# Quantizing the last two weight strips half by half, and another order of ScalarE's and GpSimd's work per strip

## The chip, the cores and the metric

The kernel runs on one core of one Trainium2 chip. The metric is device time in microseconds (us) of one execution, the median of three runs. Engines are called TensorE (PE in the profile, with PEld for its weight loads), VectorE (DVE), ScalarE (ACT), GpSimd (POOL) and SyncE (SP, which issues most DMAs). Each engine works through its own instructions strictly in the order in which they were emitted: an instruction that waits holds up everything behind it on its engine.

## The reference, cut to what matters

```python
delta = lora_B @ lora_A * 0.5                        # rank 64
scale = exp(scale_log)
normalized = ((weight + delta).reshape(O, 16, 128)) / scale
cb = codebook / max(abs(codebook), 1e-8)             # 32 entries
idx = searchsorted((cb[:-1] + cb[1:]) * 0.5, normalized, side="left")
quantized = cb[idx]
w_q = ((quantized - normalized) + normalized) * scale
w_eff = w_q + delta
h = x @ w_eff.T                                      # x: 4096 x 2048
out = x + h @ W_base.T + b_base + mixture_of_low_rank_experts(h)
```

All is float32. The kernel never forms `h`. It multiplies the quantized weight with `W_base` (and with the small router and low-rank matrices) first, and then applies the combined 2048 x 2048 matrix to `x`.

## The kernel before, in words

**Stage A** (lines 390 to 870) makes the combined matrix. The quantized weight is worked in 16 strips of 128 input columns; a strip is a tile `w` of 128 x 2048 numbers, two halves `f` of 1024. For one strip `i`:

- `delta(i, f)` (line 405): TensorE makes the low-rank half into PSUM tile `d`. There is one such tile, so the second half waits until ScalarE has read the first.
- `scaled(i, f)` (line 502, ScalarE) copies `d` into `a`, scaled. `normalize(i, f)` (lines 506 and 429, GpSimd) adds it to `w` and divides by the scale. So `w` is normalized in place, and must have been loaded first (`load_w`, line 395).
- The 31 thresholds are climbed one by one; at each, `a` is raised where `w` is above the threshold. The lowest four levels are prepared one strip ahead: `scalar_level` (lines 516, 519, 521 or 524, three ScalarE steps called parts 0, 1, 2) does level 0 of both halves and level 3 of half 0; `pool_levels` (lines 534, 535, GpSimd) does levels 1 and 2 (and level 3 of half 1 for strips 1 to 5); `last_level` (line 539) adds ScalarE's level 3.
- From strip 6 on a first half-size mask (level 3 of half 1) is left to the strip itself. Then come 27 full masks, r = 4 to 30. `raise_to` (lines 549, 550): ScalarE writes a mask `above`, VectorE copies the next level into `a` where the mask is set (COPY_PREDICATED). There are four mask tiles, so ScalarE can be at most four masks ahead.
- `straight_through` (lines 572 to 574): three element-wise passes over each half on GpSimd; for the last strip on VectorE, in quarters.
- `products(i, bs, c)` (line 621) multiplies the strip with a quarter `c` of two column blocks of `W_base` on TensorE; `multiply_router`, `router_sum`, `route` are small matmuls; `keep(i, b)` (lines 654, 655) lets ScalarE empty a PSUM bank and SP store it. Three PSUM banks (tag `m`) serve these products. One strip's products run while the next strip is quantized.

The order of all this is written by hand: in iteration `i` of the strip loop, `behind(k, f, ...)` puts a step into the program right after full mask number `k` (0 to 26) of strip `i`. That fixes its place in the order of each engine that it uses. In iteration `i` the steps for strip `i+1` (scaled, normalize, levels), the products of strip `i-1` and the last quarter of strip `i-2` are placed in this way. For strips 5 to 15 GpSimd also makes sums of finished blocks (`outer_w`, `inner_pair`) that SP stores (`put`).

After the loop the last strip's products, the last stores, and sums of the last group (`late_columns` and then `last_outer`, `last_inner` on VectorE, with GpSimd issuing their DMAs) follow.

**Stage B** (from line 873) is 196 product steps on TensorE of some 7 us each, and takes the rest of the time. It begins with VectorE still working on the last group's sums.

In the profile lines are those of the helper, not of the place in the order. The places are these, for a normal strip:

```python
behind(4, scaled, i + 1, 0)
behind(4, normalize, i + 1, 0)
behind(10, scaled, i + 1, 1)
behind(10, normalize, i + 1, 1)
for r, f, parts in ((0, 0, (11, 12, 13)), (NL - 1, 0, (14, 15, 18)), (0, 1, (19, 20, 21))):
    for n, p in enumerate(parts):
        behind(p, scalar_level, i + 1, f, r, n)
behind(14, pool_levels, i + 1, 0)
behind(19, last_level, i + 1, 0)
behind(21, pool_levels, i + 1, 1)
```

Of the kernel before, what the change touches and what calls it, by code (L numbers as in the profile page):

```python
# [13 lines left out]
U8 = mybir.dt.uint8  # L14
I32 = mybir.dt.int32
AF = mybir.ActivationFunctionType
# [5 lines left out]
P = 128  # L22
BIG = 3.0e38

GAIN = 2.0**126
# [158 lines left out]
def adaln_ffn_kernel(  # L184
# [181 lines left out]
    with ExitStack() as sa:  # L366
# [145 lines left out]
        def scalar_level(i, f, r, part):  # L512
# [9 lines left out]
            elif part == 2:  # L522
                strips[i]["lx"] = mpool0.tile([P, NM // 2, P], F32, tag="lx", name=f"lx_{i}_{f}")
                nc.scalar.activation(strips[i]["lx"], sg, AF.Copy, scale=rise[:, r : r + 1])

        def half_step(i):
            return i - 1 in made

# [12 lines left out]
        def new_mask(i, r):  # L541
            return mpool.tile([P, F], F8, tag="above", name=f"above_{i}_{r}")

        def raise_to(i, r, above, f, n):

            c = ts(f, F // n)
            q = strips[i]["w"].rearrange("p m i -> p (m i)")[:, c]
            a = strips[i]["a"].rearrange("p m i -> p (m i)")[:, c]
            nc.scalar.activation(above[:, c], q, AF.Relu, bias=neg_t[:, r : r + 1], scale=GAIN, saturate=False)  # L549
            nc.vector.copy_predicated(  # L550
                a, above[:, c].bitcast(U8), step[:, r : r + 1].to_broadcast([P, F // n])
            )

        def quantize(i, at):

            if half_step(i):
                raise_to(i, NL - 1, new_mask(i, NL - 1), 1, 2)
            for r in range(NL if i else 2, T):
                raise_to(i, r, new_mask(i, r), 0, 1)
                for do in at.pop(r - NL, []):  # L560
                    do()
            assert not at, at

        def straight_through(i):
            last = i == NS - 1
            n = 4 if last else 2
            for h in range(n):
                m = ts(h, NM // n)
                w, a = strips[i]["w"][:, m, :], strips[i]["a"][:, m, :]
                sc = scale[:, strip[i], m].unsqueeze(2).to_broadcast([P, NM // n, P])  # L570
                v = nc.vector if last else nc.gpsimd
                v.tensor_tensor(a, a, w, ALU.subtract)  # L572
                v.tensor_tensor(a, a, w, ALU.add)  # L573
                v.tensor_tensor(a, a, sc, ALU.mult)  # L574
# [70 lines left out]
        def router_parts(i):  # L645
            nc.scalar.copy(raw, strips[i]["r"][:, 0:P])

        def router_sum(i):

            nc.tensor.matmul(strips[i]["r"][:, P : P + RP], raw, stack, start=True, stop=True)  # L650

        def keep(i, b):
            out = spool.tile([P, 4, BC], F32, tag="out", name=f"out_{i}_{b}")
            nc.scalar.copy(out.rearrange("p q c -> p (q c)"), strips[i][b])  # L654
            (nc.scalar if i == NS - 1 else nc.sync).dma_start(wc_dram[i // 4][b][:, i % 4], out)

        def keep_router(i):
            nc.scalar.copy(rac[:, strip[i], :], strips[i]["r"][:, P : P + RP])
# [83 lines left out]
        def products(i, bs, c):  # L742

            for b in bs:
                multiply(i, b, c)
            if c == NC - 1:
                low_rank(i, bs)
# [7 lines left out]
        for i in range(NS):  # L755
            at = {}

            def behind(r, f, *args):
                at.setdefault(r, []).append(lambda: f(*args))

            if i > 1:

                products(i - 2, (3, 1), NC - 1)
                route(i - 2, 0)
                behind(0, load_route, i - 2, 1)
                behind(2, keep, i - 2, 3)
                behind(3, keep, i - 2, 1)
            if i + 1 < NS:
                delta(i + 1, 0)
                if i > 0:  # L770
                    behind(1, load_w, i + 1, 2)
                behind(4, scaled, i + 1, 0)
                behind(4, normalize, i + 1, 0)
                behind(10, scaled, i + 1, 1)
                behind(10, normalize, i + 1, 1)
                for r, f, parts in ((0, 0, (11, 12, 13)), (NL - 1, 0, (14, 15, 18)), (0, 1, (19, 20, 21))):
                    for n, p in enumerate(parts):
                        behind(p, scalar_level, i + 1, f, r, n)
                behind(14, pool_levels, i + 1, 0)
                behind(19, last_level, i + 1, 0)  # L780
                behind(21, pool_levels, i + 1, 1)
            if i > 0:


                behind(9, load_route, i - 1, 0)
                if i == NS - 1:
                    behind(9, load_route, i - 1, 1)
                for c in range(2):
                    behind(2 + 3 * c, products, i - 1, (2, 0), c)
                if i + 1 < NS:  # L790
                    behind(7, delta, i + 1, 1)
                if i > 1:
                    behind(8, route, i - 2, 1)
                for c in range(2, NC):
                    behind(2 + 3 * c, products, i - 1, (2, 0), c)
                behind(13, multiply_router, i - 1)
                behind(16, keep, i - 1, 2)
                behind(17, keep, i - 1, 0)
                for c in range(NC - 1):
                    behind((17, 20, 22)[c], products, i - 1, (3, 1), c)  # L800
                behind(19, router_sum, i - 1)
                behind(23, keep_router, i - 1)
                behind(18, router_parts, i - 1)
                if i + 2 < NS:
                    behind(20, load_la, i + 2)
            else:
                behind(3, nc.vector.reciprocal, rflat[:, NM:], flat[:, NM:])
                behind(7, delta, i + 1, 1)
                behind(22, lora_columns, 0)
                behind(24, lora_columns, 1)  # L810
                behind(25, lora_router)
            for n, (g, b) in enumerate(made.get(i, [])):
                step_of = (3, 5, 10, 13, 17, 23, 25) if len(made[i]) == 1 else (
                    (4, 6, 8, 9, 10, 12, 13) if n == 0 else (17, 19, 21, 22, 23, 24, 25)
                )

# [21 lines left out]
                behind(r[5], put, g, b, PAIRS[2])  # L838
                behind(r[6], put, g, b, PAIRS[3])
            quantize(i, at)  # L840
            straight_through(i)

        last = NS - 1
        products(last - 1, (3, 1), NC - 1)
# [10 lines left out]
        for bs in ((2, 0), (3, 1)):  # L855
            for c in range(NC):
                products(last, bs, c)
            if bs[0] == 2:
                multiply_router(last)
                router_parts(last)  # L860
            for b in bs:
                keep(last, b)
            if bs[0] == 2:
                router_sum(last)
                keep_router(last)
                late_columns()
        for h in range(2):
            route(last, h)
        for h in range(2):
# [336 lines left out]
    def do(where, n):  # L1206
        for g in range(NG):
            for f, args in where.get(n - NP * g, []):
                f(g, *args)
# [71 lines left out]
```

## Time and profile before

| what | value |
|---|---|
| time, median of 3 runs | 2667.78 us (2667.24 to 2671.78) |
| the profiled execution's own time | 2666.77 us |
| its span | 2665.0 us |
| stage A, until TensorE's first stage B matmul | 0 to 1244.6 us |
| GpSimd starts the straight-through of strip 0, 5, 13 | 100.74, 457.08, 1030.03 us |
| VectorE begins the last strip's straight-through | 1172.56 us |

Busy time by stretch, in us (the stretch 743 to 815 is about one strip; 1240 to 2665 is stage B):

| stretch | length | PE | DVE | ACT | POOL |
|---|---|---|---|---|---|
| 243 to 314 | 71 | 65.11 | 66.75 | 64.55 | 54.38 |
| 743 to 815 | 72 | 66.53 | 68.37 | 66.24 | 63.76 |
| 1180 to 1240 | 60 | 54.15 | 13.16 | 1.52 | 26.29 |
| 1240 to 2665 | 1425 | 1414.81 | 421.47 | 76.78 | 376.56 |

A line of the timeline reads: start and length in us, engine, line of the kernel, operation, what is written from what, shapes, how many such instructions in a row, and in brackets how long the engine stood idle before it and what ended that.

### The profile page before, as it was taken

To read this page: it belongs to the slowest core of one execution; us is meant where nothing else is said; L and a number is where in the kernel's file an instruction comes from. 1 tells how busy PE (TensorE), PEld (TensorE's weight loads), DVE (VectorE), ACT (ScalarE), POOL (GpSimd) and SP (SyncE) were. 2 spreads that over 40 slices of the span, in tenths; PEclk is the share of its full clock that TensorE was granted. 3 is DMA by queue.
4 is the path that set the end of the run, shared out by engine and by line. 5 is a ranking of instruction groups with operands and counts; after the bars stand their busy time and mean duration, and the time that the engine had idled before them with its cause. 6 is when DMAs were issued, how large, how long until landed. Compare 5 with 4: busy or idle time off the path is not lost.

```text
span 2665.0 us, 26423 instructions
## 1 busy us (share of the span) xinstructions
PE 2503.9 (94%) x10576; PEld 1704.1 (64%) x10576; DVE 1549.0 (58%) x990; ACT 1130.1 (42%) x796; POOL 1367.2 (51%) x783
## 2 busy tenths in 40 slices
PE   5499999999999999999999999999999999999999
PEld 2244444444444444345888888888888888888887
DVE  9999999999999999973433223242133332224221
ACT  7899999999999999930000000000000000000000
POOL 5777778889888888745313140042320323202224
PEclk9799999999999999999999999999999999999999
DMA  8255457776777777699844666536675455854554
GB/s 317 102 177 185 168 181 252 233 241 228 234 243 249 235 231 227 217 327 347 323 174 173 218 245 232 187 142 213 244 234 194 157 206 177 279 208 173 194 199 158
DMA packets 225979, 581.08 MB, mean 218 GB/s; under 512 B 20600, under 2 KB 121728, under 8 KB 182720
## 3 DMA queue, kind: packets, MB, share of 16 engines
q1 hardware_dynamic: 219296, 557.96, 61.1%
q0 software_dynamic: 4960, 14.95, 1.6%
q10 hardware_dynamic: 1600, 6.49, 0.7%
q8 instruction: 83, 1.36, 0.2%
q14 instruction: 40, 0.33, 0.0%
HBM read 477.62 MB, written 101.71 MB: 217 GB/s over the span
## 4 chain that ended last, share of the span: by engine, by line
PE 62%; ACT 17%; DVE 8%; POOL 7%; DMA 3%; issue 2%; SPq 0%; DVEq 0%; ACTq 0%; POOLq 0%
PE z L954 49%; ACT above L549 11%; PE m L621 10%; DVE a L550 7%; ACT sg L516 2%; ACT sg L519 2%; POOL a L572 1%; POOL a L573 1%; PE z L984 1%; ACT a L521 1%; POOL lv L534 1%; POOL a L574 1%; POOL a L535 1%; DMA xA<-in_xT 1%; DMA wc_dram<-out 1%
## 5 line engine op out<-in xcount | busy, mean ns | idle before, releaser
L550 DVE COPY_PREDICATED a<-above,step 128x2048 f32<-128x2048 uint8 (+1 forms) x448 | 1090.2, 2436 | 61.1 <-ACT above L549 19.3
L549 ACT ACTIVATE above<-w,neg_t 128x2048 fp8e5<-128x2048 f32 (+1 forms) x448 | 872.4, 1976 | 55.1 <-DVE a L550 44.5
L954 PE MATMUL z<-t,s 128*128 128x256 f32 x3584 | 791.4, 380 | 2.0 <-DVE u L1036 1.7
L954 PEld LDWEIGHTS z<-t,s 128*128 128x128 f32 x3584 | 677.5, 190 | 105.5 <-issue 13.2
L621 PE MATMUL m<-wbp,a 128*128 128x512 f32 x1024 | 502.1, 636 | 115.0 <-POOL a L574 101.0
L621 PE MATMUL m<-wb,a 128*128 128x512 f32 x1024 | 462.1, 594 | 4.4 <-ACT out L654 4.4
L621 PEld LDWEIGHTS m<-wbp,a 128*128 128x128 f32 x1024 | 202.6, 204 | 370.9 <-issue 239.7
L621 PEld LDWEIGHTS m<-wb,a 128*128 128x128 f32 x1024 | 194.5, 191 | 247.1 <-issue 242.4
L1034 ACT COPY m<-z 128x1024 f32<-128x1024 f32 x28 | 28.4, 1013 | 759.2 <-PE z L954 759.2
L1045 POOL TENSOR_TENSOR c<-u,m 128x1024 f32<-128x1024 f32 x16 | 50.1, 3130 | 443.8 <-DVE u L1042 422.4
L954 PE MATMUL z<-xA,s 128*128 128x256 f32 x1152 | 254.6, 379 | 0.0
L534 POOL TENSOR_SCALAR lv<-w,past,rise 128x1024 f32<-128x1024 f32 x65 | 245.9, 3783 | 3.7
L954 PEld LDWEIGHTS z<-xA,s 128*128 128x128 f32 x1152 | 218.8, 190 | 30.5 <-issue 0.8
L1045 POOL TENSOR_TENSOR M<-u,m 128x1024 f32<-128x1024 f32 x8 | 24.5, 3068 | 328.9 <-DVE u L1042 288.2
L954 PE MATMUL z<-xC,s 128*128 128x256 f32 x768 | 169.7, 379 | 0.0
L954 PE MATMUL z<-xB,s 128*128 128x256 f32 x768 | 169.7, 379 | 0.0
L535 POOL TENSOR_TENSOR a<-a,lv 128x1024 f32<-128x1024 f32 x65 | 154.3, 2374 | 27.1 <-ACT a L521 21.0
L1036 DVE TENSOR_TENSOR u<-z,m 128x1024 f32<-128x1024 f32 x28 | 34.3, 1224 | 218.5 <-issue 175.0
L1040 ACT COPY m<-z 128x1024 f32<-128x1024 f32 x28 | 28.3, 1011 | 308.8 <-PE z L954 308.8
L954 PEld LDWEIGHTS z<-xC,s 128*128 128x128 f32 x768 | 145.9, 190 | 19.8
L954 PEld LDWEIGHTS z<-xB,s 128*128 128x128 f32 x768 | 145.9, 190 | 19.8
L1042 DVE TENSOR_TENSOR u<-z,u 128x1024 f32<-128x1024 f32 x28 | 34.3, 1223 | 119.8 <-PE z L954 81.3
(213 smaller groups left out, 1958.0 us busy)
## 6 DMA issues: line engine op xcount, KB each, us to landing
s<-s_dram SPq DMA_DIRECT2D x196, 1024.0 KB, 4.9
wbp<-in_wbT SPq DMA_DIRECT2D x131, 1024.0 KB, 5.4
xs<-in_xT SPq DMA_DIRECT2D x64, 512.0 KB, 6.5
xA<-in_xT SPq DMA_DIRECT2D x24, 1024.0 KB, 9.4
s_dram<-z SPq DMA_DIRECT2D x84, 256.0 KB, 6.2
xB<-in_xT SPq DMA_DIRECT2D x16, 1024.0 KB, 10.4
outT<-M SPq DMA_DIRECT2D x16, 1024.0 KB, 12.5
w<-in_weight SPq DMA_DIRECT2D x30, 512.0 KB, 5.2
```

Of the source, the lines that this page charges most:

```text
L516: nc.scalar.activation(strips[i]["sg"], q, AF.Relu, bias=neg_t[:, r : r + 1], scale=GAIN)
L519: nc.scalar.activation(sg, sg, AF.Sign)
L534: v.tensor_scalar(lv, half(i, f, "w"), past[:, r : r + 1], rise[:, r : r + 1], ALU.is_gt, ALU.mult)
L535: v.tensor_tensor(a, a, lv, ALU.add)
L549: nc.scalar.activation(above[:, c], q, AF.Relu, bias=neg_t[:, r : r + 1], scale=GAIN, saturate=False)
L550: nc.vector.copy_predicated(a, above[:, c].bitcast(U8), step[:, r : r + 1].to_broadcast([P, F // n]))
L621: nc.tensor.matmul(ps, strips[i]["a"][:, CM * c + m, :], t[:, m, :], start=c == 0 and m == 0, stop=False)
L954: nc.tensor.matmul(z[:, c, :], s[:, k, ts(c, P)], rhs[:, k, :], start=not more and k == 0 and c % PER == 0, stop=k == NK - 1 and c % PER = ...
L1034: nc.scalar.copy(temp("m1", o), z["a"])
L1036: nc.vector.tensor_tensor(temp("u2", o), z["b"], state["m1", o], ALU.add)
L1042: nc.vector.tensor_tensor(temp("u3", o), z["d"], state["u2", o], ALU.add)
L1045: lambda d: nc.gpsimd.tensor_tensor(d, state["u3", o], state["m5", o], ALU.add),
```

## The change

Three things are changed. The computation is the same.

1. **ScalarE's and GpSimd's steps for the next strip stand at other places**, and `delta(i+1, 1)` moves from place 7 to place 1, in front of the strip's product blocks. `keep` of strip `i-2` moves from places 2 and 3 to 0 and 2; `keep(i-1, 0)`, `router_parts`, `router_sum` and `keep_router` move one place back. GpSimd's sums of finished blocks move from (3, 5, 10, 13, 17, 23, 25) to (5, 12, 14, 16, 23, 24, 25).
2. **Strips 14 and 15 are quantized half by half**: 27 half-size masks for half 0, its straight-through on GpSimd, then 28 for half 1. Two half masks share one mask tile, and a place `k` now comes after each pair. Half 1 of strip 15 has its straight-through on VectorE in two quarters.
3. **Behind the loop** the last strip's PSUM banks are emptied (`evacuate`) directly after their products, and the stores, `router_sum` and `late_columns` come after the first quarter of the second pair of blocks.

```diff
+        HALVED = NS - 2
-        def raise_to(i, r, above, f, n):
+        def raise_to(i, r, above, f, n, at=None):
             c = ts(f, F // n)
...
+            above = above[:, ts(f if at is None else at, F // n)]
+            nc.scalar.activation(above, q, AF.Relu, bias=neg_t[:, r : r + 1], scale=GAIN, saturate=False)
+            nc.vector.copy_predicated(a, above.bitcast(U8), step[:, r : r + 1].to_broadcast([P, F // n]))
...
+        def halves(i, at):
+            n = 0
+            for f in range(2):
+                for k in range(T - NL + f):
+                    r = NL - f + k
+                    if n % 2 == 0:
+                        mask = new_mask(i, f"{f}{r}")
+                    raise_to(i, r, mask, f, 2, n % 2)
+                    n += 1
+                    if n % 2 == 0:
+                        for do in at.pop(n // 2 - 1, []):
+                            do()
+                if i == NS - 1 and f == 1:
+                    straight_through(i, f, nc.vector, 2)
+                else:
+                    straight_through(i, f, nc.gpsimd, 1)
...
-                behind(2, keep, i - 2, 3)
-                behind(3, keep, i - 2, 1)
+                behind(0, keep, i - 2, 3)
+                behind(2, keep, i - 2, 1)
...
-                behind(4, scaled, i + 1, 0)
-                behind(4, normalize, i + 1, 0)
-                behind(10, scaled, i + 1, 1)
-                behind(10, normalize, i + 1, 1)
-                for r, f, parts in ((0, 0, (11, 12, 13)), (NL - 1, 0, (14, 15, 18)), (0, 1, (19, 20, 21))):
+                behind(1, scaled, i + 1, 0)
+                behind(1, delta, i + 1, 1)
+                behind(3, scaled, i + 1, 1)
+                for f in range(2):
+                    behind(4, normalize, i + 1, f)
+                for r, f, parts in ((0, 0, (7, 9, 10)), (0, 1, (12, 14, 15)), (NL - 1, 0, (19, 20, 22))):
...
-                behind(14, pool_levels, i + 1, 0)
-                behind(19, last_level, i + 1, 0)
-                behind(21, pool_levels, i + 1, 1)
+                behind(10, pool_levels, i + 1, 0)
+                behind(15, pool_levels, i + 1, 1)
+                behind(22, last_level, i + 1, 0)
...
-                if i + 1 < NS:
-                    behind(7, delta, i + 1, 1)
...
-                behind(17, keep, i - 1, 0)
+                behind(18, keep, i - 1, 0)
...
         for bs in ((2, 0), (3, 1)):
             for c in range(NC):
                 products(last, bs, c)
+                if bs[0] == 3 and c == 0:
+                    router_sum(last)
+                    keep_router(last)
+                    for b in (2, 0):
+                        store(last, b, nc.scalar)
+                    late_columns()
             if bs[0] == 2:
                 multiply_router(last)
-                router_parts(last)
+            for b in bs:
+                evacuate(last, b)
+            if bs[0] == 2:
+                router_parts(last)
...
+        for b in (3, 1):
+            store(last, b, nc.scalar)
```

## The prediction

> **What bounds the kernel.** I read the page's 40 slices first (VectorE at 9 up to about 1175 us, then TensorE alone at 9), then the chain of waits, then the timelines of single engines around one strip. Write t for the moment at which VectorE ends a strip's last full mask; GpSimd's straight-through starts then, VectorE goes on with the next strip.
>
> ```profile
> L550 DVE COPY_PREDICATED a<-above,step 128x2048 f32<-128x2048 uint8 x434 | 1072.9, 2472 | 60.9 <-ACT above L549 19.3 <-DVE a L550 2.3 <-ACT raw L646 0.5
> ...
> 173.46 69.44 DVE L550 COPY_PREDICATED a<-above,step 128x2048 f32<-128x2048 uint8 x27 [0.19 <-ACT above L549]
> ...
> 730.71 65.61 DVE L550 COPY_PREDICATED a<-above,step 128x2048 f32<-128x2048 uint8 x26 [0.56 <-ACT above L549]
> 796.53 2.46 DVE L550 COPY_PREDICATED a<-above,step 128x2048 f32<-128x2048 uint8 x1 [0.22 <-ACT above L549]
> 799.37 2.47 DVE L550 COPY_PREDICATED a<-above,step 128x2048 f32<-128x2048 uint8 x1 [0.38 <-ACT above L549]
> 802.40 29.42 DVE L550 COPY_PREDICATED a<-above,step 128x2048 f32<-128x2048 uint8 x12 [0.56 <-ACT above L549]
> ```
>
> VectorE does 27 masks in 69.44 us: 2.576 us from one start to the next. 65.61 us hold 25 such and one half mask, so that one took 1.32. Unhindered, strips 1 to 5 need 69.6 us and strips 6 to 14 70.9. GpSimd's straight-through starts (100.74, 457.08, 1030.03, 1101.59) give 71.3 and 71.6. All waits of VectorE for ScalarE in stage A are 19.3 us: no reordering can win more than some 20 us there.
>
> Why it waits: ScalarE runs ahead and gains 0.67 per mask (1.90 against 2.576), and loses each step placed between masks (1.04, 0.95, 1.13 for the three parts of a level, 0.47 a keep, 0.9 a scaled).
>
> ```profile
> 743.53 2.39 POOL L572 TENSOR_TENSOR a<-a,w 128x1024 f32<-128x1024 f32 x1 [5.88 <-DVE a L550]
> ...
> 768.23 1.02 ACT L502 ACTIVATE a<-d 128x1024 f32<-128x1024 f32 x1 [3.48 <-PE d L410]
> 769.15 1.99 ACT L549 ACTIVATE above<-w,neg_t 128x2048 fp8e5<-128x2048 f32 x1
> 771.04 1.14 ACT L516 ACTIVATE sg<-w,neg_t 128x1024 bf16<-128x1024 f32 x1
> ```
>
> In this strip (t = 743.5) mask 11 ends at 771.1 and VectorE wants it at 743.5 + 1.32 + 11 x 2.576 = 773.1: 2.0 ahead. Up to mask 22 ScalarE gains 11 x 0.67 = 7.4 and loses 10.4: VectorE should wait 0.9 in all. The three waits above sum to 1.16. The count holds, so I use it for the new order.
>
> **The new order: a new wait at place 7.** The change takes away the 3.48 us wait (delta half 1 now runs in TensorE's idle time before the products) and spreads the steps. But `scalar_level(i+1, 0, 0)` part 0 moves from place 11 to 7. It reads normalized `w`, and the loads of `w` are not moved:
>
> ```profile
> 254.62 0.80 SPq L395 DMA_DIRECT2D w<-in_weight  x2
> ...
> 259.41 2.38 POOL L506 TENSOR_TENSOR w<-w,a 128x1024 f32<-128x1024 f32 x1 [2.85 <-DMA w<-in_weight]
> 261.87 1.90 POOL L429 TENSOR_TENSOR w<-w,rscale 128x1024 f32<-128x1024 f32 x1
> ```
>
> Here t is 243.0. SP may load `w` only when the straight-through's second half has read the old one (t + 11.6; 755.16 = t + 11.7 in the later strip). GpSimd begins at t + 16.4 and half 0 is normalized at t + 20.8. From strip 5 on GpSimd had its block sums before that; they now come behind, so it waits for the load in every strip. ScalarE, stopped behind mask 7, ends part 0 at t + 21.8 and mask 8 at t + 23.85. VectorE wants mask 8 at t + 20.6 (strips 1 to 5) or t + 1.32 + 8 x 2.576 = t + 21.9. So **it waits 3.2 or 1.95 us per strip**, with masks 8 and up queued behind part 0 on ScalarE. From mask 8 the count goes +0.67, +0.39, -0.08, and stays positive: the old late waits are gone, and a strip is 23.9 + 19 x 2.576 = 72.8 us.
>
> - Strips 1 to 5: 356.3 before. In strip 1 the load was there at t + 15.6, so 72.0 + 4 x 72.8 = 363.2: **+6.9**.
> - Strips 6 to 13: 573.0 before, 8 x 72.8 = 582.4: **+9.5**.
>
> Here a rule would give another answer. The Trainium skill ("DMA: Bandwidth & Descriptors", Anatomy of one DMA) prices a DMA at about 2.0 us plus bytes over 436 GB/s, fitted on the GpSimd path: 3.2 us for half of `w`, against 4.8 (254.62 to 259.41) here beside other loads. By the rule 13 strips would each be 1.6 us shorter and the whole about 2667, no change. The row decides: same load, same place.
>
> Other moves. `keep(i-2, 3)` at place 0 waits for TensorE's low-rank matmuls, which end up to 2 us after t; mask 1 queues behind it. That costs up to 0.7 at mask 1, but the wait at mask 8 is fixed from t and swallows it. SP's store, fetch and load behind it still go out before t + 11.6. GpSimd's order, summed from its rows (normalize to t + 25, sums 5.1, two levels 12.6, pairs 5.8, two levels 12.6, last level 2.4, pairs 4.7), ends near t + 68, before the next straight-through; in strips 1 to 5 it no longer ends at t itself as at 243.0. Those I cost at nothing.
>
> **Halves.** The trace has 14 half masks, mean 1317 ns, plus some 0.09 us to the next start: 1.40. The Trainium skill ("Perfetto Trace Analysis", Optimizing Scalar/DVE Operations) counts some 60 ns per extra VectorE instruction and says that grouping helps a saturated engine: 27 x 0.06 = 1.6 us a strip. The rows say more: two halves 2.80 for one full 2.576. Bounds for the step: 1.29 (half of a full one) to 1.42. Strip 14: 55 x 1.40 = 77.0, and 0.5 at place 7 (22.9 against 16 x 1.40), 77.5 against 71.56: **+5.9** (0 to +7). Strip 15 gets 77 too, but there TensorE is the later one, as follows.
>
> **The end.** TensorE before: last strip's products from 1175.21, t + 73.6 for that strip (t = 1101.6), to 1244.6, t + 143.
>
> ```profile
> 1175.21 3.67 PE L621 MATMUL m<-wbp,a 128*128 128x512 f32 x8 [1.76 <-issue]
> ...
> 1215.74 5.40 PE L621 MATMUL m<-wb,a 128*128 128x512 f32 x8 [4.43 <-ACT out L654]
> ...
> 1288.53 7.17 PE L954 MATMUL z<-t,s 128*128 128x256 f32 x32 [1.71 <-DVE u L1036]
> ```
>
> After, half 0 of strip 14 is ready early and TensorE starts its products some 10 us sooner, but then stands at a full PSUM: the second pair needs `keep(14, 2)`, still at place 16, which ScalarE, at most 8 half masks ahead, reaches near t + 39. From there 30 us of products and 2 of route end at t + 73: as before. Strip 15's own products then go on without a stop, since half 0 is ready and VectorE ends half 1 at t + 80, before TensorE wants it at t + 87. Their matmuls are 69.4 less the stalls at 1215.74 (4.43, and 1.8 for the slow matmuls after it), the wait for raw and half the one for wbp: 62.5. End t + 135.6: **-7.3**. It is partly given back. The two stores leave 24 us before the end instead of 29.4, behind the first quarter of the second pair; the late sums, GpSimd's 28 issues and VectorE's last sums follow one after another, and the wait of 1.71 at 1288.53 grows by that: **+5.9** (0 if slack lies in that chain).
>
> **Sum:** 6.9 + 9.5 + 5.9 - 7.3 + 5.9 = +20.9. On the profiled execution (2665.0 span, 2666.8 with what lies around it) 2687.7; the median is 1.0 above that: **2688**.
>
> **Rivals.**
> - *The order works (faster).* If half 0 is normalized by t + 18.9, mask 8 is in time; that needs the load 2 us sooner than any seen. Then strips 1 to 13 fall to VectorE's floor, 5 x 69.6 + 8 x 70.9 = 915 for 929, strip 14 costs 5.4, the end gives 1.4: 2657. For it: ScalarE is busy 66 of 71.6 us, enough if spread. Against: three loads arrived at t + 15.6 to 16.4.
> - *Half of it.* The load comes 1 us sooner, or the end keeps its 7.3: about 2676.
> - *TensorE takes over.* The keeps at 16 and 18 hold its PSUM; by my count its cycle closes at t + 6.5, and the straight-through lets it go at t + 6.9. If it slips by 2 us, strips become 74.3: 2707.
>
> **Chances.** Forecast 0.72, the order works 0.10, half of it 0.10, TensorE 0.08. Within 0.2% (5.3 us, what a measurement here can tell from none) lies only the low edge of the middle case: faster 0.10, same 0.05, slower 0.85. Range 2671 to 2700: loads 4.3 to 6.0 us after issue, the half step's bounds and the give-back of 0 to 5.9; it leaves out the fast and the TensorE rival.
>
> **What would show it.** ScalarE's L516 idle before it, released by GpSimd's w, in each of strips 1 to 14; VectorE waiting 2 to 3 us for one mask per strip and hardly else; strips 72.8 apart; half masks 1.40 apart in strip 14; TensorE without a stop from strip 15's first product to stage B; a longer wait for `u` early in stage B. Strips of 71 us or less would prove the main step wrong.

## The result, and the profile after

The changed kernel takes **2695.47 us** (median of 4 runs, 2694.36 to 2699.24) where the kernel before takes 2669.78 (median of 4, 2667.24 to 2675.93): the ratio is 1.0095, with a 95% interval of 1.0074 to 1.0117. It is slower by about 1%. The profiled execution has a span of 2694.2 us against 2665.0.

First the page of the kernel before, TensorE's base products, then that of the kernel after: VectorE's masks and TensorE's base products. The columns are busy time and mean ns of one, then the idle time just before them and what ended most of it.

```profile
L621 PE MATMUL m<-wbp,a 128*128 128x512 f32 x1024 | 502.1, 636 | 115.0 <-POOL a L574 101.0
```

```profile
L554 DVE COPY_PREDICATED a<-above,step 128x2048 f32<-128x2048 uint8 (+1 forms) x502 | 1097.1, 2189 | 91.8 <-ACT above L553 42.9
...
L645 PE MATMUL m<-wbp,a 128*128 128x512 f32 x1024 | 504.5, 639 | 96.7 <-ACT out L678 89.8
```

VectorE's waits for a mask have grown from 19.3 to 42.9 us. TensorE's idle time before its products is somewhat smaller (96.7, 115.0 before), but something else ends it: formerly the straight-through on GpSimd (101.0), now ScalarE's evacuation of a PSUM bank (89.8). The waits view of the kernel after, from the start to 1280 us (who waited, for whom, us in total, times, longest), shows a ring of such waits:

```profile
ACT out L678 <- PE m L633: 139.5, 17, 29.5
...
PE m L645 <- ACT out L678: 89.8, 15, 8.2
...
DVE a L554 <- ACT above L553: 42.9, 34, 4.2
...
POOL w L506 <- DMA w<-in_weight: 36.3, 12, 4.1
ACT sg L516 <- POOL w L429: 31.1, 15, 8.0
```

ScalarE waits for TensorE, TensorE for ScalarE (a ring: each hands its lateness on to the other, from strip to strip), ScalarE for GpSimd's `w` and GpSimd for the load of `w`. One strip of the kernel after, with t = 758.56, from the timeline:

```profile
758.56 2.36 POOL L596 TENSOR_TENSOR a<-a,w 128x1024 f32<-128x1024 f32 x1 [4.76 <-DVE a L554]
...
762.39 0.59 ACT L678 COPY out<-m 128x512 f32<-128x512 f32 x1 [6.35 <-PE m L633]
...
764.91 2.48 DVE L554 COPY_PREDICATED a<-above,step 128x2048 f32<-128x2048 uint8 x1 [2.65 <-ACT above L553]
767.72 15.40 DVE L554 COPY_PREDICATED a<-above,step 128x2048 f32<-128x2048 uint8 x6 [0.32 <-ACT above L553]
...
776.24 2.38 POOL L506 TENSOR_TENSOR w<-w,a 128x1024 f32<-128x1024 f32 x1 [4.11 <-DMA w<-in_weight]
...
780.63 1.15 ACT L516 ACTIVATE sg<-w,neg_t 128x1024 bf16<-128x1024 f32 x1 [2.09 <-POOL w L429]
...
783.70 48.88 DVE L554 COPY_PREDICATED a<-above,step 128x2048 f32<-128x2048 uint8 x19 [0.58 <-ACT above L553]
...
804.53 5.39 PE L645 MATMUL m<-wbp,a 128*128 128x512 f32 x8 [6.04 <-ACT out L678]
```

VectorE waits at two masks: 2.65 us at mask 1, which ScalarE makes only after an evacuation that waited 6.35 us for TensorE's low-rank matmuls, and 0.58 at mask 8, which stands behind the step that wants `w` (L516). At the end of the strip TensorE stands 6.04 us for the evacuation at place 16. And the end of stage A, from the same view:

```profile
1057.76 2.73 DVE L554 COPY_PREDICATED a<-above,step 128x1024 f32<-128x1024 uint8 x2 [2.92 <-ACT above L553]
1060.75 149.32 DVE L554 COPY_PREDICATED a<-above,step 128x1024 f32<-128x1024 uint8 x106 [0.26 <-ACT above L553]
...
1172.04 5.95 PE L645 MATMUL m<-wbp,a 128*128 128x512 f32 x8 [8.20 <-ACT out L678]
...
1205.31 3.70 PE L645 MATMUL m<-wbp,a 128*128 128x512 f32 x8
...
1266.40 7.17 PE L987 MATMUL z<-xA,s 128*128 128x256 f32 x32
...
1315.60 9.32 PE L987 MATMUL z<-t,s 128*128 128x256 f32 x32 [6.66 <-DVE u L1069]
```

The half masks are (149.32 - 1.3) / 105 = 1.41 us apart. Stage B begins at 1266.40, where it began at 1244.58 before. The matmul that waits for `u` comes at 1315.60 instead of 1288.53: `u` is the step by which VectorE empties a PSUM tile of stage B, and VectorE comes to it only behind the late sums of stage A's last group.

The table has the parts of the trace for all kernels below. A strip's length is the distance between GpSimd's straight-through starts (line 572 before, 596 after); "t15" is such a start, at the end of strip 14 (where strip 14 is in halves, that of its second half); "A ends" is TensorE's first matmul of stage B, "u" the matmul that waits for `u`. All in us.

| kernel | median | ratio, 95% interval | strips 1-5 | 6-13 | 14 | t15 | A ends | u |
|---|---|---|---|---|---|---|---|---|
| before | | | 356.3 | 573.0 | 71.6 | 1101.6 | 1244.6 | 1288.5 |
| after | 2695.5 | 1.0095 [1.0074, 1.0117] | 364.0 | 587.6 | 80.5 | 1132.8 | 1266.4 | 1315.6 |
| 1 keeps at 2, 3 | 2696.7 | 1.0091 [1.0078, 1.0105] | 366.1 | 587.0 | 80.5 | 1134.3 | 1267.9 | 1317.6 |
| 2 levels late | 2661.9 | 0.9959 [0.9945, 0.9973] | 349.6 | 568.6 | 78.0 | 1097.0 | 1230.1 | 1280.9 |
| 3 keeps at 14, 16 | 2692.8 | 1.0074 [1.0062, 1.0087] | 365.7 | 587.0 | 78.1 | 1131.6 | 1259.7 | 1312.3 |
| 4 old order | 2672.4 | 1.0003 [0.9995, 1.0011] | 356.6 | 573.0 | 78.0 | 1108.5 | 1241.8 | 1293.1 |
| 5 first level at 9 | 2663.3 | 0.9967 [0.9954, 0.9979] | 351.5 | 568.9 | 77.8 | 1098.9 | 1232.0 | 1282.4 |
| 6 stores sooner | 2662.6 | 0.9964 [0.9952, 0.9977] | 351.2 | 568.8 | 78.1 | 1099.1 | 1232.6 | 1282.8 |
| 7 only 15 in halves | 2658.6 | 0.9954 [0.9941, 0.9966] | 350.8 | 568.8 | 70.9 | 1091.3 | 1231.7 | 1285.5 |
| 8 no halves | 2659.4 | 0.9951 [0.9938, 0.9965] | 351.2 | 568.8 | 70.9 | 1091.8 | 1229.9 | 1281.2 |
| 9 stores at once | 2661.2 | 0.9961 [0.9948, 0.9975] | 351.1 | 569.2 | 78.0 | 1099.2 | 1232.5 | 1280.3 |
| 10 both of 8 and 9 | 2660.2 | 0.9961 [0.9949, 0.9974] | 350.9 | 569.2 | 70.9 | 1091.7 | 1234.2 | 1280.4 |
| 11 old end | 2661.6 | 0.9966 [0.9953, 0.9978] | 351.4 | 568.7 | 70.9 | 1092.1 | 1236.7 | 1282.8 |
| 12 low-rank half alone | 2659.9 | 0.9951 [0.9938, 0.9965] | 349.2 | 569.0 | 70.9 | 1089.7 | 1235.9 | 1281.5 |

The kernel before was run again beside each group of these: medians 2671.5 (1 to 4), 2671.9 (5 to 8), 2670.8 (9 to 11) and 2671.8 (12). Its one profiled execution (2666.8) lies 4 to 5 us below these, so traces are compared by their parts here, and totals by the ratios.

### The profile page after: what moved, and what is told of

The parts are those of the page before. It is cut to its first block, busy times and chain, and to the rows that moved or that the text cites. A ratio compares the mean times of both kernels' runs of the same rounds, so it can differ in the third digit from the quotient of the medians.

```text
span 2694.2 us, 26529 instructions
## 1 busy us (share of the span) xinstructions
PE 2507.1 (93%) x10576; PEld 1707.0 (63%) x10576; DVE 1553.9 (58%) x1038; ACT 1134.1 (42%) x850; POOL 1372.9 (51%) x786
## 4 chain that ended last, share of the span: by engine, by line
PE 61%; DVE 15%; ACT 12%; POOL 6%; DMA 3%; issue 2%; DVEq 0%; SPq 0%; POOLq 0%; ACTq 0%
PE z L987 49%; DVE a L554 13%; PE m L645 9%; ACT above L553 9%; DMA w<-in_weight 2%; POOL a L597 2%; POOL a L596 2%; PE z L1017 1%; ACT sg L516 1%; POOL w L506 1%; POOL w L429 1%; ACT sg L519 1%; POOL a L598 1%; ACT a L521 1%; DMA s_dram<-late 1%
## 5 line engine op out<-in xcount | busy, mean ns | idle before, releaser
L554 DVE COPY_PREDICATED a<-above,step 128x2048 f32<-128x2048 uint8 (+1 forms) x502 | 1097.1, 2189 | 91.8 <-ACT above L553 42.9
L645 PE MATMUL m<-wbp,a 128*128 128x512 f32 x1024 | 504.5, 639 | 96.7 <-ACT out L678 89.8
L1078 POOL TENSOR_TENSOR c<-u,m 128x1024 f32<-128x1024 f32 x16 | 49.8, 3113 | 444.0 <-DVE u L1075 422.7
L596 POOL TENSOR_TENSOR a<-a,w 128x1024 f32<-128x1024 f32 x31 | 73.5, 2370 | 109.5 <-DVE a L554 109.5
```

The lines of the kernel that those rows point to most:

```text
L554: nc.vector.copy_predicated(a, above.bitcast(U8), step[:, r : r + 1].to_broadcast([P, F // n]))
L645: nc.tensor.matmul(ps, strips[i]["a"][:, CM * c + m, :], t[:, m, :], start=c == 0 and m == 0, stop=False)
L1078: lambda d: nc.gpsimd.tensor_tensor(d, state["u3", o], state["m5", o], ALU.add),
```

## The experiments

Two theories fit this profile. **A**, the prediction's: the step at place 7 wants a `w` that is not normalized yet. **B**, near the prediction's third rival: the evacuations at 16 and 18 hold TensorE's PSUM, so its low-rank matmuls end late (at t + 3.8 in the strip above) and the evacuation at place 0 waits for them. The trace of after shows both waits, and cannot say which of them feeds the other.

### 1 to 3: each link of the ring opened by itself

```diff
-                behind(0, keep, i - 2, 3)
-                behind(2, keep, i - 2, 1)
+                behind(2, keep, i - 2, 3)
+                behind(3, keep, i - 2, 1)
```

> The changed kernel, with keep(i-2, 3) and keep(i-2, 1) back at places 2 and 3. Theory A (the step at place 7 wants a w that is not normalized yet, as the prediction had it): the wait at mask 1 goes, but mask 8 is late instead, by 2 to 3 us where it was 0.3 to 1.0; strips 6 to 13 take 72.8 each where they took 73.45, and the median falls by 3 to 9 us, to 2687-2692. Theory B (TensorE is held by the evacuations at 16 and 18, so its low-rank halves end at t + 3.8 and the evacuation at place 0 waits for them): ScalarE meets that wait no more, mask 8 stays at 1 us or less, strips take 71.6 to 72.2, and the median falls by 18 to 27 us, to 2669-2678.

No change: ratio 1.0091. Both theories missed: the wait at mask 1 went neither to mask 8 nor away, but to masks 2 and 4. Timeline of this kernel, t = 760.08:

```profile
765.96 1.02 ACT L502 ACTIVATE a<-d 128x1024 f32<-128x1024 f32 x1 [6.48 <-PE d L410]
...
768.90 5.07 DVE L554 COPY_PREDICATED a<-above,step 128x2048 f32<-128x2048 uint8 x2 [2.53 <-ACT above L553]
...
805.46 5.63 PE L645 MATMUL m<-wbp,a 128*128 128x512 f32 x8 [5.78 <-ACT out L678]
```

ScalarE no longer waits in the evacuation, but in the next step that needs TensorE (L502, place 1), which TensorE does after the same late low-rank matmuls. The evacuation at place 0 is only where the lateness showed.

```diff
-                for r, f, parts in ((0, 0, (7, 9, 10)), (0, 1, (12, 14, 15)), (NL - 1, 0, (19, 20, 22))):
+                for r, f, parts in ((0, 0, (11, 12, 13)), (NL - 1, 0, (14, 15, 18)), (0, 1, (19, 20, 21))):
...
-                behind(10, pool_levels, i + 1, 0)
-                behind(15, pool_levels, i + 1, 1)
-                behind(22, last_level, i + 1, 0)
+                behind(14, pool_levels, i + 1, 0)
+                behind(19, last_level, i + 1, 0)
+                behind(21, pool_levels, i + 1, 1)
```

> The changed kernel, with ScalarE's three levels of the next strip and GpSimd's levels back at their places of before (11 to 21; 14, 19, 21), all evacuations left at 0/2 and 16/18. Theory A: nothing waits for w at place 7, so VectorE's wait for ScalarE shrinks to under 1 us a strip and the median falls by 12 to 20 us, to 2676-2684. Theory B: the evacuation at place 0 still waits for TensorE and mask 1 is still 1 to 4 us late; only the 0.3 to 1.0 us at mask 8 go, and the median falls by at most 8 us, to 2687-2696.

It takes 2661.9 us, 33.6 less than the changed kernel and less than before too (ratio 0.9959). That is more than theory A allowed, and theory B, which expected at most 8, falls as a cause of its own. From the page of this kernel VectorE's group, then a line of its waits view (0 to 1280):

```profile
L554 DVE COPY_PREDICATED a<-above,step 128x2048 f32<-128x2048 uint8 (+1 forms) x502 | 1098.7, 2192 | 54.4 <-ACT above L553 3.8
```

```profile
PE m L645 <- ACT out L678: 27.3, 17, 10.8
```

The waits for masks are 3.8 us in all where they were 42.9. TensorE's waits for evacuations went from 89.8 to 27.3 as well, though the evacuations are still at 16 and 18: they were a consequence.

```diff
-                behind(16, keep, i - 1, 2)
-                behind(18, keep, i - 1, 0)
+                behind(14, keep, i - 1, 2)
+                behind(16, keep, i - 1, 0)
```

> The changed kernel, with keep(i-1, 2) and keep(i-1, 0) at places 14 and 16 instead of 16 and 18. Theory B: TensorE's wait of 6 us before the second pair of products falls to about 1 us, its low-rank halves end before or at t, ScalarE doesn't wait at place 0, the wait at mask 1 goes, and the median falls by 15 to 27 us, to 2669-2681. Theory A: TensorE comes earlier all the same, but VectorE's wait moves from mask 1 to mask 8 (2 to 3 us there), and the median falls by 3 to 9 us, to 2687-2692.

2692.8 us: theory A's case (2687 to 2692), less than 1 us above it. Timeline of this kernel, t = 760.26:

```profile
776.29 2.37 POOL L506 TENSOR_TENSOR w<-w,a 128x1024 f32<-128x1024 f32 x1 [2.49 <-DMA w<-in_weight]
...
780.67 1.15 ACT L516 ACTIVATE sg<-w,neg_t 128x1024 bf16<-128x1024 f32 x1 [6.51 <-POOL w L429]
...
783.75 20.57 DVE L554 COPY_PREDICATED a<-above,step 128x2048 f32<-128x2048 uint8 x8 [1.76 <-ACT above L553]
804.64 29.48 DVE L554 COPY_PREDICATED a<-above,step 128x2048 f32<-128x2048 uint8 x12 [0.33 <-ACT above L553]
...
805.13 3.70 PE L645 MATMUL m<-wb,a 128*128 128x512 f32 x8 [1.09 <-ACT out L678]
```

and of its waits view (0 to 1280):

```profile
ACT sg L516 <- POOL w L429: 96.2, 15, 8.0
...
DVE a L554 <- ACT above L553: 40.7, 31, 3.6
...
PE m L645 <- ACT out L678: 25.7, 16, 7.1
```

With TensorE let go (its waits for evacuations are 25.7 instead of 89.8) nothing stops ScalarE before place 7, and there it waits 6.51 us. Over the stage ScalarE's wait for `w` triples, from 31.1 to 96.2, and VectorE loses as much as ever, now at mask 8. Here the predicted wait stands nearly alone: part 0 begins at t + 20.4, mask 8 reaches VectorE at t + 23.5, 1.76 late (prediction: t + 20.8, t + 23.85, 1.95). Over strips 6 to 13 VectorE's wait at mask 8 is 1.7 to 2.3 us, 1.92 in the mean; another 0.66 a strip stands at masks 15 and 16 (0.33 above), which ScalarE makes among the second level's parts and an evacuation.

### 4: the halves and the end alone

The kernel before in the order of its strips, with the halves and the new end: every `behind` line of the change is taken back, among them

```diff
-                behind(1, scaled, i + 1, 0)
-                behind(1, delta, i + 1, 1)
-                behind(3, scaled, i + 1, 1)
-                for f in range(2):
-                    behind(4, normalize, i + 1, f)
+                behind(4, scaled, i + 1, 0)
+                behind(4, normalize, i + 1, 0)
+                behind(10, scaled, i + 1, 1)
+                behind(10, normalize, i + 1, 1)
...
+                    behind(7, delta, i + 1, 1)
```

> The kernel before in the order of all its strips, with two parts of the change alone: the last two strips in halves, and the new order of the last strip's evacuations and stores. If the order is what lost 15 to 23 us up to strip 14, strips 1 to 13 are those of before (71.6 each), strip 14 takes 77.5 without its first wait of 2.9, the end of stage A comes 130 to 135 us after the start of strip 15's straight-through step, and the median is 2664-2674, within 6 us of before. If the gain of 9.4 us at the end of stage A needs the new order (its low-rank halves and products being ahead), that end stays at 143 after it, and the median is 2674-2682.

2672.4 us, ratio 1.0003 (0.9995 to 1.0011): the two other parts of the change together are worth nothing that could be measured (-1.3 to +2.9 us), and the order accounts for the loss of 23.1 us (2695.5 - 2672.4). Strip 14 takes 78.0 without the wait of 2.92 at its first mask, and stage A ends 133.4 us after t15 where it was 143.0, so that gain does not need the new order.

### 5: the first level two places later

After experiments 1 to 3 the theory was A2: ScalarE is stopped at place 7, so it comes late to 16 and 18, so TensorE ends late, so ScalarE is late again at the next strip's place 0. Its rival C held the second level's parts at 12 to 15, in front of the evacuation at 16, to be what keeps TensorE waiting. The smallest edit that tells them apart moves part 0 of the first level by two places, its parts 1 and 2 by one, and with them GpSimd's levels, which add to what part 2 writes:

```diff
-                for r, f, parts in ((0, 0, (7, 9, 10)), (0, 1, (12, 14, 15)), (NL - 1, 0, (19, 20, 22))):
+                for r, f, parts in ((0, 0, (9, 10, 11)), (0, 1, (12, 14, 15)), (NL - 1, 0, (19, 20, 22))):
...
-                behind(10, pool_levels, i + 1, 0)
+                behind(11, pool_levels, i + 1, 0)
```

> The changed kernel, with ScalarE's first level alone moved back by two places and less (parts at 9, 10, 11 instead of 7, 9, 10; GpSimd's levels of that half at 11 instead of 10). Theory A2 (ScalarE's stop before its first level is the cause, and TensorE's wait for its PSUM buffers follows from it, because a ScalarE that was stopped comes late to places 16 and 18): at place 9 the normalized w is there or nearly, ScalarE's waits for w fall from 31 us in all to under 12, TensorE's for the evacuations from 90 to under 50, strips 6 to 13 take 70.9 to 71.6, and the median falls to 2662-2676. Theory C (the second level's parts at 12 to 15, in front of the evacuation at 16, hold TensorE): TensorE's wait of 6 us a strip stays, and the median stays within 8 us of the changed kernel's 2695.

2663.3 us: this small delay is worth 32.2 us, and C falls. Timeline of this kernel, t = 736.72:

```profile
734.20 74.62 DVE L554 COPY_PREDICATED a<-above,step 128x2048 f32<-128x2048 uint8 x30
...
752.61 2.38 POOL L506 TENSOR_TENSOR w<-w,a 128x1024 f32<-128x1024 f32 x1 [2.34 <-DMA w<-in_weight]
...
757.00 1.15 ACT L516 ACTIVATE sg<-w,neg_t 128x1024 bf16<-128x1024 f32 x1 [0.79 <-POOL w L429]
```

The load is as late as in experiment 3 (GpSimd begins at t + 15.9, part 0 at t + 20.3), and ScalarE still waits 0.79 for it. But the mask behind part 0 is now mask 10. It is ready 1.15 + 2.0 us later, at t + 23.4; VectorE wants it at t + 1.32 + 10 x 2.576 = t + 27.1. Mask 8 was wanted at t + 21.9. The 30 masks of the first line run without a stop.

### 6 to 11: why the end gives nothing

All of these have the levels at their places of before, as in experiment 2. Experiment 6 moves the last strip's stores of blocks 2 and 0 ahead of the router's sum:

```diff
                 if bs[0] == 3 and c == 0:
+                    for b in (2, 0):
+                        store(last, b, nc.scalar)
                     router_sum(last)
                     keep_router(last)
-                    for b in (2, 0):
-                        store(last, b, nc.scalar)
                     late_columns()
```

> The kernel with the levels at their places of before (2661.9), and in the last strip the stores of blocks 2 and 0 issued ahead of the router's sum and its evacuation, which ScalarE's queue now reaches only after a wait of 7.2 us for TensorE. If that queueing is what gives the gain at the end of stage A back: the stores go out 7 us earlier, VectorE's wait for the late columns shrinks from 37.7 to about 30, TensorE's wait for u (7.6) goes with the slower matmuls behind it (9.9 instead of 7.2), and the median falls by 5 to 10 us, to 2652-2657. If another transfer holds u (the chunks of the last columns, stored at the very end of the stage), the wait stays and the median is within 2 us of 2661.9.

2662.6: a miss. The stores had not stood behind the router's evacuation alone, but also behind the issue of a `wbp` load: they went out at 1205.8 instead of 1206.7 (3.4 us sooner, counted from the evacuations, which came later in this execution). Experiment 9 puts them right behind the evacuations:

```diff
                     keep_router(last)
-                    for b in (2, 0):
-                        store(last, b, nc.scalar)
                     late_columns()
...
             for b in bs:
                 evacuate(last, b)
             if bs[0] == 2:
+                for b in bs:
+                    store(last, b, nc.scalar)
                 router_parts(last)
```

> The kernel with the levels at their places of before (2661.9), and the last strip's stores of blocks 2 and 0 issued by ScalarE right behind their evacuations, ahead of the base block's load for the second pair of products, whose issue waits 3.6 us for its buffer and stood in front of the stores in the kernel that moved them less. If the late stores are what gives the gain at the end of stage A back, the stores go out 6 to 7 us earlier than at 1206.7, the late columns' chain on VectorE and GpSimd and the wait for u move with them, the end of stage A stays at 1230, and the median falls by 5 to 9 us, to 2653-2657. If the wait for u hangs on the last columns' own transfers, it is within 2 us of 2661.9.

2661.2, within 2 us of 2661.9: a miss of the main expectation again, though the stores went out at 1200.8 and 1204.8 now. First three lines of experiment 2's timeline, then of experiment 9's:

```profile
1197.89 1.07 ACT L678 COPY out<-m 128x512 f32<-128x512 f32 x2 [29.55 <-PE m L633]
...
1206.69 0.82 ACTq L682 DMA_DIRECT2D wc_dram<-out  x2
...
1217.13 2.62 DVE L320 TENSOR_TENSOR late<-late 128x512 f32<-128x512 f32 x4 [37.66 <-DMA late<-wc_dram]
```

```profile
1200.23 1.07 ACT L678 COPY out<-m 128x512 f32<-128x512 f32 x2 [29.55 <-DMA xA<-in_xT]
...
1200.84 4.31 ACTq L682 DMA_DIRECT2D wc_dram<-out  x2
...
1216.88 2.62 DVE L320 TENSOR_TENSOR late<-late 128x512 f32<-128x512 f32 x4 [35.60 <-DMA late<-wc_dram]
```

In experiment 9's execution strip 15 ran some 2 us later already (t15 1099.2 against 1097.0), with nothing changed before it, so the two are counted from the evacuation (L678). From there the stores are issued 8.2 and 4.6 us sooner, but VectorE's first late sum comes only 2.6 us sooner (16.65 instead of 19.24). The windows view of experiment 9 (stretch, length, busy time and count of PE, PEld, DVE, ACT and POOL, granted clock, DMA share, GB/s) shows what the stores met:

```profile
1200.00:1205.00 5.00, 5.00 (x45) 2.62 (x44) 0.00 (x0) 1.07 (x2) 4.79 (x7) 1.00 1.03 381
1205.00:1210.00 5.00, 5.00 (x16) 2.51 (x15) 0.00 (x0) 0.45 (x2) 0.02 (x1) 1.00 1.08 385
1210.00:1215.00 5.00, 5.00 (x13) 2.24 (x12) 0.00 (x0) 0.00 (x0) 0.00 (x0) 1.00 0.89 297
```

The 16 DMA engines are full until 1210. From issue to landing the stores took 6.9 and 8.3 us. In experiment 2 the engines were as full until 1210, then emptied (share 0.34 from 1210 to 1215), and the second store, issued at 1207.1, took 5.6. So part of the lead went in the transfers; that the full engines are the reason is likely, but not shown: in experiment 6 a store issued at 1206.9 took 8.0. And 2.6 us is less than the medians can tell (the interval of experiment 9's ratio is 0.0027 wide, 7 us).

Experiments 7 and 8 take halves away. Experiment 7:

```diff
-        HALVED = NS - 2
+        HALVED = NS - 1
```

> The kernel with the levels at their places of before (2661.9), with strip 15 alone in halves. Halves of strip 14 cost VectorE 6.5 to 7 us and give TensorE strip 14's first half 33 us earlier. If TensorE has no use for it (it stops 10.8 us for the evacuation at place 16 of strip 15 in any case), strip 15 starts 7 us earlier and the median falls by 3 to 7 us, to 2655-2659. If TensorE needs it, strip 14's products end later by as much as they start later, and the median is 2660-2668.

Experiment 8, in which strip 15's straight-through goes back to VectorE:

```diff
-        HALVED = NS - 2
+        HALVED = NS
...
-                straight_through(i, f, nc.gpsimd, 1)
+                straight_through(i, f, nc.vector if i == NS - 1 else nc.gpsimd, 2 if i == NS - 1 else 1)
```

> The kernel with the levels at their places of before (2661.9), with no strip in halves and the last straight-through step on VectorE as before. Strip 14 takes 71 instead of 78, strip 15's masks 71 instead of 77, but its first half is quantized at the same moment as its second. If the halves are what brings strip 15's products forward, the end of stage A stands at 140 to 143 us after the start of strip 15 (133 with halves), and the median is within 4 us of 2661.9; if the new order of evacuations does it alone, that end stays at 133 to 136, and the median is 2653-2658.

2658.6 and 2659.4. Both are at most 3.3 us below 2661.9, with overlapping intervals. In 8 the end of stage A comes 138.2 us after t15, between the two cases expected. The halves bring it forward by 5 us and cost strip 14 7.1 (78.0 - 70.9).

Experiment 10 is 8 with the edit of 9. Experiment 11 is 8 with the lines behind the loop as before:

```diff
-            store(i, b)
+            store(i, b, nc.scalar if i == NS - 1 else nc.sync)
...
-                if bs[0] == 3 and c == 0:
-                    router_sum(last)
...
             if bs[0] == 2:
                 multiply_router(last)
+                router_parts(last)
             for b in bs:
-                evacuate(last, b)
+                keep(last, b)
             if bs[0] == 2:
-                router_parts(last)
+                router_sum(last)
+                keep_router(last)
+                late_columns()
```

> The kernel with no strip in halves and the levels at their places of before (2659.35), and the last strip's stores of blocks 2 and 0 issued right behind their evacuations. By the same reading the stores' 7 us come on top of what leaving out the halves gave, and the median is 2650-2655; if the late stores are not what holds u, 2657-2661.

> The kernel with no strip in halves and the levels at their places of before (2659.35), and with the last strip's evacuations and stores in the order of the kernel before. It is then the new order of strips 1 to 13 alone. If the new order of the last strip gains nothing in the end (its earlier end of stage A is given back as a longer wait for u), the end of stage A is 3 to 5 us later than 138 after the start of strip 15, stage B is 1420-1424 instead of 1429, and the median is 2652-2659. If it does gain, the median is 2663-2667.

2660.2 and 2661.6. Stores at once show no gain in the median without halves either, and here too one execution cannot say why: in 10 TensorE stood 4.18 us for a load of `wbp` (1.69 in 8) before the last strip's first pair of blocks was done, closed that pair 4.3 us later than in 8, and met `u` 79.7 us behind it instead of 84.7.

With the end of before, stage A ends 144.6 us after t15 instead of 138.2, and yet the median differs by only 2.3 us. The table says why. In experiments 2, 5, 6 and 8 to 12, t15 lies between 1089.7 and 1099.2 and the end of stage A between 1229.9 and 1236.7, but the matmul that waits for `u` comes at 1280.3 to 1282.8, and the span ends 1378 to 1379 us later. (In experiment 7 it comes at 1285.5, in an execution of 2665.1 us, 6.5 above that kernel's median.) It hangs on the chain of late sums that starts when TensorE has finished strip 15's first pair of blocks. In experiment 2 that pair closes at 1196.7, the first late sum follows at 1217.1 (above), and VectorE then stands for the sums' own stores and fetches until it comes to `u`:

```profile
1253.76 1.23 DVE L965 TENSOR_TENSOR t<-t,xA 128x1024 f32<-128x1024 f32 x1 [14.48 <-DMA s_dram<-late_z]
...
1266.68 2.62 DVE L320 TENSOR_TENSOR last<-last 128x512 f32<-128x512 f32 x4 [7.69 <-DMA last<-wc_dram]
...
1279.61 1.22 DVE L1069 TENSOR_TENSOR u<-z,m 128x1024 f32<-128x1024 f32 x1
...
1280.88 9.91 PE L987 MATMUL z<-t,s 128*128 128x256 f32 x32 [7.60 <-DVE u L1069]
```

From the pair's closing to the `u` matmul it is 84 to 87 us in 2, 5, 6, 8, 11 and 12, 81.2 and 79.7 in 9 and 10 with their early stores, 84.5 before and 82.6 after. So what comes behind that pair, the end of stage A above all, is waited away. The halves cancel in front of it: without them (8) the pair closes 104.7 us after t15, with them (2) 99.7, but t15 is 5.2 us later.

### 12: one part of the order alone

The kernel before, with only the low-rank half moved:

```diff
-                behind(4, scaled, i + 1, 0)
+                behind(1, scaled, i + 1, 0)
+                behind(1, delta, i + 1, 1)
+                behind(3, scaled, i + 1, 1)
...
-                behind(10, scaled, i + 1, 1)
...
-                    behind(7, delta, i + 1, 1)
```

> The kernel before with one part of the new order alone: the second half of the next strip's low-rank product at place 1 instead of 7, and the two copies of it by ScalarE at places 1 and 3 instead of 4 and 10; everything else, normalization at 4 and 10 too, as before. Strips 1 to 13 took 71.3 and 71.6 each before and 69.9 and 71.1 in the new order without its early first level. If that gain comes from the low-rank halves being ahead of the strip's blocks (ScalarE's 50 us of waits for that product gone), strips 1 to 5 take 69.7 to 70.4, strips 6 to 13 70.9 to 71.2, and the median is 2660-2665. If the evacuations' new places (0 and 2, 16 and 18) are needed for it, ScalarE waits for TensorE at place 1 or 3 instead, and the median is 2668-2675.

2659.9 us, ratio 0.9951 (0.9938 to 0.9965). From the page of this kernel VectorE's masks, then ScalarE's waits for the low-rank product from the waits view (0 to 1280), before and in this kernel:

```profile
L550 DVE COPY_PREDICATED a<-above,step 128x2048 f32<-128x2048 uint8 (+1 forms) x448 | 1091.3, 2439 | 48.2 <-DVE a L550 2.3
```

```profile
ACT a L502 <- PE d L410: 49.8, 14, 5.5
```

```profile
ACT a L502 <- PE d L410: 28.6, 13, 4.2
```

VectorE's waits for masks have left the line (1.7 us in all, 19.3 before); strips 6 to 13 take 71.1 us each and strip 14 70.9, where unhindered ones need 70.9. ScalarE's waits for the low-rank product fell from 49.8 to 28.6 us. This version, a few lines against the kernel before, is as fast as the best of the others; among 2 and 5 to 12 the intervals don't tell one from another. Which of its three moves does it was not separated.

## Why the prediction was right, and where its sizes were off

- **The new wait at place 7** (predicted +6.9 and +9.5, chance 0.72) is shown to be the cause, by experiments 2 and 5. Its own clockwork is confirmed by experiment 3 (mask 8 late by 1.92 in the mean of strips 6 to 13, 1.95 predicted). Measured were +7.6 in strips 1 to 5 and **+14.6 in strips 6 to 13**, 73.45 a strip instead of 72.8.
- **The mis-sized term** is the sentence on `keep(i-2, 3)`, "up to 0.7 at mask 1, but the wait at mask 8 is fixed from t and swallows it". In strips 6 to 13 mask 1 was 1.0 to 3.0 us late, 2.0 in the mean, and it is mask 8's wait that was swallowed (0.4 in the mean). The sum stopped at mask 8 and let ScalarE be in time from there. It left out that a ScalarE stopped in place 7 comes late to 16, where TensorE stands for it (6.04), and that TensorE hands this on to the next strip. Taken by itself that link is no cause: undone in experiment 3, it gave 2.7 us in the median and almost nothing in strips 6 to 13 (587.0 for 587.6), because the wait at mask 8 then came in full and the 0.66 at masks 15 and 16 with it. So "TensorE takes over" (0.08) named a wait that came, but not what decides; its 74.3 us a strip were not reached in the mean.
- **The load of `w`**: t + 16.4 predicted for GpSimd's start; in strips 6 to 13 it was t + 16.0 to 16.5 in experiment 3 and t + 16.0 to 17.7 in the kernel after. In the two strips shown SP issued it at t + 11.6 (771.85 and 770.18), and it took 4.4 and 6.1 us; 4.3 in experiment 5. The row's 4.8 was right to be taken, and not the estimate of 3.2 that the Trainium skill ("DMA: Bandwidth & Descriptors", Anatomy of one DMA) leads to. In the strip of after, the fetch of finished blocks, which SP does behind the late evacuation's store, went out 5.5 us before the load (764.72), in experiment 3 11.5 us before (760.35); that this made the difference was not tested.
- **What was hidden under it**: the prediction knew that the 3.48 us wait goes and that strips 1 to 13 could then fall by 14 us in all, from 929 to 915 ("the order works"). Experiment 2 has 918.2. Two places for one step decided between 2663.3 and 2695.5 (experiment 5); the price of that rival, 2657, was good, and its chance of 0.10 rested on the right condition.
- **Halves**: the half step, 1.40 predicted, is 1.41. Strip 14 took 80.5 instead of 77.5, of which 2.92 is the ring's wait at its first mask; without it 78.0 (experiments 2 and 4).
- **The end**: strip 15's products were to begin at t15 + 73 and end at t15 + 135.6; they began at t15 + 72.5 and ended at t15 + 133.6, so the gain was 9.4, not 7.3. The give-back was 7.4 in stage B (predicted 5.9). The bound of the prediction was right, "the late sums follow one after another". But halves and end together were summed to +4.5, and measured alone they are +0.85 (-1.3 to +2.9, experiment 4).

That the measured +25.7 is close to the predicted +20.9 is thus one right mechanism, undersized by some 8 us over strips 6 to 14, less some 4 us for halves and end; that these two errors partly cancel is luck. The total alone would show neither: by its interval it is +20 to +31 us. The sizes come from the parts of single executions.

What stays open: why the load of `w` took up to 6.1 us in the kernel after, and what the stores at once are worth, whose gain of 2.6 us in one trace is below what the medians tell. Place 8 for the first level was not tried. Nor was the `wbp` traffic moved that fills the DMA engines when the last stores go out.

## What to carry to other kernels

When a step on an in-order engine is moved forward, compare two moments: when its input is ready, and when the consumer runs out of the work that stands before the step. Two places (5.2 us) were here the difference between a wait that nobody notices and a kernel that is 1.2% slower (2663.3 against 2695.5). A wait that shows up all round a ring of engines may have one place where it enters, as here; opening the ring elsewhere only moved the wait, and the edit that told was the one that delayed the suspected step, not those that helped its victims. And before the end of a stage is shortened, look for the chain that the next stage waits for: eight kernels with ends of stage A up to 7 us apart met `u` within 2.6 us of each other.

## What the runs showed of the hardware

- In experiment 9 two stores of 256 KB issued into DMA engines at a share of 1.03 to 1.08 took 6.9 and 8.3 us to land, and in experiment 2 one issued 4.6 us later (counted from the evacuation), with a share of 0.34 at its end, 5.6. Of the 4.6 us lead 2.6 were left at the reader.
- A mask of half the size takes 1.41 us from start to start on VectorE against 2.576 for the whole: two halves cost 9% more than one full mask. Strip 14 takes 78.0 us in halves and 70.9 without.
- In experiment 9 the second of two stores issued by ScalarE went out 4.0 us behind the first (1204.8 and 1200.8), though the copy that it stores had ended at 1201.3. What held it is not shown by these runs.
